# Cross-attention and FP4 FFN on one core: O evicted by VectorE without bias products, eight residual adds and three strips on GpSimd, Sqrt table ahead of Va

## The chip, the cores and the metric

The kernel runs on one core of a Trainium2 chip. The metric is the device time of one execution in microseconds, and the time before is the median of three runs. The engines are named as in the profile: PE (TensorE), DVE (VectorE, `V` in the code), ACT (ScalarE, `A`), POOL (GpSimd, `G`) and SP (SyncE, which here only issues DMAs).

## The reference

The input is 64 sequences of 128 positions with 256 features. With x and the context ctx, both f32, the reference is in short:

```python
# attention over time shifts, weights shared by all sequences
q, k, v = (layernorm(x) @ Wq + bq), (ctx @ Wq + bq), (ctx @ Wq + bq)   # 16 features each
corr = mean(ifft(fft(q) * conj(fft(k))))            # one number per shift
w, shift = softmax(top_k(corr, 12))
R = sum_i w_i * roll(v, -shift_i)                   # along the 128 positions
x = x + repeat(R, 16 heads) @ Wout + bout
# FFN with blockwise FP4 quantisation (blocks of 16 along the last axis)
n = layernorm(x)
h = silu(fp4(n) @ fp4(w_gate).T) * (fp4(n) @ fp4(w_up).T)      # 704 wide
x = x + fp4(h) @ fp4(w_down).T
```

`fp4` divides each block of 16 by its largest magnitude over 6 (but not by less than 1e-12), snaps to the FP4 grid and multiplies back. The top-k takes floor(2 ln 512) = 12 shifts. The attention's result does not depend on all 64 sequences separately: the heads repeat one head, so what is added to x before the FFN is, per group of rows, one 128x256 matrix O.

## The kernel before, in words

**Layout.** The 8192 rows are 64 tiles of 128 rows and 256 features. Four tiles make a quad `X[q]` (128x4x256, f32), loaded by one DMA; quad q has its own `O[q % 4]`, so there are four matrices O, each 128x257 (the last column is a row mean for the layer norm).

**Stages.** Until about 53 us the context, x and the weights are loaded, q, k and v are projected and correlated, and the weights are quantised. Then comes the transition that the change is about, and from 72 us the FFN of tile after tile.

**The transition.** Top-k and softmax run on DVE. ACT fetches the exponentials `E`. The shift weights are turned into a matrix `Wp` (two halves, 128x257): half 0 is started by DVE, half 1 by ACT (L1552, `t1_op`), and both are finished by DVE (L1559). The projected values are transformed by PE into the PSUM tile `pa` and copied by ACT to `Va`, one copy of 128x256 for each of the four groups (L1504). Before the change the planner lets ACT load the Sqrt table (L1553) behind the first of these copies. Then O[g] = Va[g] times Wp over the sum of the exponentials (`inv`), plus the output bias `Bo`:

- O[0] is two matmuls into `pdc` (L1581) and an eviction on DVE that multiplies by `inv` and adds `Bo` (L1594).
- O[1] to O[3] begin with a product of `es` with `Bo` (L1572), a matmul with one row that puts the bias times the sum of exponentials into PSUM, and go on with the two matmuls (L1581). ACT evicts them with the scale `inv` (L1588). All three use the tile `pa`, at other offsets.

**From O to the FFN's input (`x_parts`, L426).** For quad q: `neg` is the negative row mean (L461); the residual X += O is added (L447 on DVE, two tiles at a time; for quads from 3 on, L483, a DMA from the GpSimd queue that accumulates in memory, one for each tile); `cc` = X + neg (L499 on ACT). The first two tiles (`fast`) take cc = X + neg + O in one DVE instruction (L472) and have the add behind it. Then the squares are summed (L509 on ACT), block maxima `am` taken (L519 on DVE), the roots computed (two Sqrt on ACT, L535 and L542, for quads 0 and 1; a polynomial on DVE, L408 to L424, for the others), `am` is floored and scaled (L552, L562), cc multiplied by the reciprocals (L586), snapped to the grid (`k`, L594 or L600 and L607, then L338), and split in two f16 parts `xhl` (L573, L579, L615). `xhl` is transposed to `xT`: for quad 0 by PE with a copy by DVE (tiles 0, 1) or ACT (tiles 2, 3) (L631, L637), for the others by a DMA (L644).

**The FFN of a tile (`group_ops`).** Eighteen matmuls (L1224) make gate and up in one of two PSUM tiles `pg` (called `gu` in the profile), ACT takes silu(gate) (`g`, L1230), DVE multiplies by up (`h`, L1237), reduces block maxima (`hs`, L1247) and their reciprocals (`hr`, L1261), GpSimd multiplies h by hr (`z`, L1276; tiles 0, 62 and 63 on DVE), ACT rounds (L1304, L1320), DVE snaps (L338) and makes the two f16 parts `hl` (L1329), a DMA transposes them, PE multiplies by the down weights (L1373, L1375), DVE adds to X (L1392), and a DMA stores. The reduction for hs also reads two strips beside h in the same tile, 2x88 columns filled once with the least scale (`least`): before the change ACT writes them, once for each of the three buffers of h (L1605).

**What sets the order.** All instructions are first noted by `op(engine, cost, function, reads, writes, dl=...)`, where cost is the author's estimate in ns and `dl` a due time; then a list scheduler (class `Order`) picks, on each engine, among the instructions that are ready the one due first, and writes them out. Each engine executes its list in that order, and waits by semaphores. A due time is handed back to all that an instruction depends on, so a change of one cost or due time shifts the order later on too. `chain` forces an instruction to follow another on the same engine at once: from tile 2 on, hr of tile t-1, h and hs of tile t come one after another on DVE, and the z of tile t-1 on GpSimd, which waits for that hr, runs beside that h and hs. `after` orders without a wait. PSUM waits are per tile: an instruction that writes any part of `pa` waits for earlier readers of `pa`.

On GpSimd the list before is short: after the set-up come the DMAs that accumulate O in quads 3 and 4 (five issues between 73.5 and 78.1 us), then z of tile 1, and from there a z and an accumulating DMA for a later tile (`BEFORE` = 16 tiles ahead) in turn.

Of the kernel before, what the change touches and what calls it, by code (L numbers as in the profile page):

```python
# [18 lines left out]
AF = mybir.ActivationFunctionType  # L19
ALU = mybir.AluOpType  # L20
# [3 lines left out]
P = 128  # L24
D = 256
NF = 704
NB = NF // 16
# [65 lines left out]
class Order:  # L93
# [11 lines left out]
    def op(self, eng, cost, fn, r=(), w=(), dl=1e9, lat=0, after=(), rel=0.0, port=True, late=0.0):  # L105


        o = Op()
        o.port, o.chain, o.late = port, None, late
        o.eng, o.cost, o.fn, o.dl, o.lat, o.n = eng, cost, fn, dl, lat, len(self.ops)  # L110
        o.rel = max(rel, self.rel)
        o.deps, o.succ, o.end, o.bufs, o.after = set(), [], None, set(), set(after)
        for k in r:
            if k in self.last_w:
                o.deps.add(self.last_w[k])
        for k in w:
            if k in self.last_w:
                o.deps.add(self.last_w[k])
            o.deps.update(self.readers.get(k, ()))
        for k in r:  # L120
            self.readers.setdefault(k, set()).add(o)
        for k in w:
            self.last_w[k] = o
            self.readers[k] = set()
        for k in (*r, *w):
            b = k[0] if isinstance(k, tuple) else k
            if isinstance(b, Buf) and b not in o.bufs:
                o.bufs.add(b)
                b.ops.append(o)
        o.deps.discard(o)  # L130
        self.ops.append(o)
        return o
# [128 lines left out]
def xattn_ffn(ctx: ExitStack, tc: tile.TileContext, x, xt, cx, wo, bo, wgu, wd, out):  # L261
    nc = tc.nc
    PE, V, A, G, SP = nc.tensor, nc.vector, nc.scalar, nc.gpsimd, nc.sync
# [4 lines left out]
    op = S.op  # L268
# [5 lines left out]
    O = [res.tile([P, D + 1], F32, name=f"O{g}") for g in range(4)]  # L274
# [59 lines left out]
    def load_x(q, **kw):  # L334
        return op("SP", 1460, lambda: SP.dma_start(X[q].t, x[:, q]), w=[(X[q], i) for i in range(4)] + (["XA"] if q in (6, 7) else []), lat=LL, **kw)
# [4 lines left out]
    SLOT = 5425.0  # L340
# [18 lines left out]
    LL = 1100.0  # L359
    LA = 4000.0  # L360
    BEFORE = 16
    HOT2 = 70000.0
    ZV, CV, EV = (0, *range(62, 64)), range(61, 64), range(64)
    HPE = (63,)
# [35 lines left out]
    def x_stage(*a, **kw):  # L400
        for _ in x_parts(*a, **kw):
            pass
# [23 lines left out]
    def x_parts(R, q, i0, nt, fast, due, alu, pe_x=False, root=False, both=None, off=0):  # L426
# [11 lines left out]
        def cv():  # L438
            return sub("k").bitcast(F16)

        eng = "V"
        pe = fast

        def add(lo, hi):
            def f():
                v = Xq.t[:, i0 + lo : i0 + hi]
                (V if eng == "V" else G).tensor_tensor(v, v, O[g][:, 0:D].unsqueeze(1).broadcast_to([P, hi - lo, D]), ALU.add)  # L447

            n = hi - lo
            op(  # L450
                eng,
                (60 + 270 * n) if eng == "V" else 650 * n if n == 1 else 613 * n,
                f,
                r=[("O", g)],
                w=[(Xq, i0 + i) for i in range(lo, hi)],
            )
# [8 lines left out]
            w=[T["neg"]],  # L465
        )
        for i in tiles:
            if fast:
                op(
                    "V",  # L470
                    336,
                    lambda i=i: V.scalar_tensor_tensor(  # L472
                        T["cc"].t[:, i], Xq.t[:, i0 + i], T["neg"].t[:, i : i + 1], O[g][:, 0:D], ALU.add, ALU.add
                    ),
                    r=[(Xq, i0 + i), T["neg"], ("O", g)],
                    w=[(T["cc"], i)],
                )
        if alu == "D":
            for i in tiles:
                adds[4 * q + i] = op(  # L480
                    "G",
                    900,
                    lambda i=i: G.dma_start(Xq.t[:, i0 + i], O[g][:, 0:D], accum_op=ALU.add),  # L483
                    r=[("O", g)],
                    w=[(Xq, i0 + i)],
                    lat=LA,
                    port=False,
                )
                adds[4 * q + i].rel = 0.0
        else:  # L490
            step = 1 if nt == 1 else 2
            for lo in range(0, nt, step):
                add(lo, lo + step)
        for i in tiles:
            if not fast:
# [702 lines left out]
    def group_ops(tiles):  # L1198
# [16 lines left out]
        for i, t in enumerate(tiles):  # L1215
# [47 lines left out]
                w=[(B["r"], i)],  # L1263
                port=False,
            )
            if t - 1 in recips:
                recips[t - 1].deps.add(g_op)
                recips[t - 1].chain, h_op.chain = h_op, red_op
                h_op.after.add(recips[t - 1])
# [152 lines left out]
    def heat_buf(buf, dl=1e9):  # L1422
        heat(lambda: buf.t[:, 0:P], buf, dl, buf)
# [129 lines left out]
    op("A", 1300, lambda: A.activation(warm, c_half, AF.Sqrt), w=["tbl"], dl=TO, after=[*quick, t1_op])  # L1553
    for e in range(2):
        key, t = spec["B", e]
        w_op = op(
# [5 lines left out]
        )  # L1562
    d_parts(loaded, (w_op,))
    load_x(1, dl=TD + 9000, after=loaded)
    for g in range(4):
        po, pn = ((pdc, "o"), lambda: pdc.t[:, 0 : D + 1]) if g == 0 else ((pa, "o", g), lambda g=g: pa.t[:, 512 * (3 - g) :][:, 0 : D + 1])
        Vg = Va[:, g].rearrange("p (b r e) -> p e (b r)", b=16, e=2)
        if g:
            op(
                "PE",  # L1570
                690,
                lambda pn=pn: PE.matmul(pn(), es[0:1, 0:1].broadcast_to([1, P]), Bo[0:1], start=True, stop=False),  # L1572
                r=["Bo", "es"],
                w=[po],
                after=quick_o,
            )
        first = [
            op(
                "PE",
                560,  # L1580
                lambda e=e, pn=pn, Vg=Vg, g=g: PE.matmul(pn(), Vg[:, e], Wp[:, e], start=(g == e == 0), stop=(e == 1)),  # L1581
                r=[("Va", g), ("Wp", e)],
                w=[po],
            )
            for e in range(2)
        ]
        if g:
            op("A", 450, lambda g=g, pn=pn: A.activation(O[g], pn(), AF.Copy, scale=inv), r=[po, "inv"], w=[("O", g)], dl=TG if g < 2 else TG + SLOT)  # L1588
        else:
            quick_o = first  # L1590
            op(
                "V",
                450,
                lambda pn=pn: V.scalar_tensor_tensor(O[0], pn(), inv, Bo, ALU.mult, ALU.add),  # L1594
                r=[po, "inv", "Bo"],
                w=[("O", 0)],
                dl=TG,
            )

    heat(lambda: hot.t[:, 384:512], (hot, "h"), TG + 7000.0, hot, after=first)  # L1600
    for t in h_tiles:
        op(
            "A",
            350,
            lambda t=t: A.activation(  # L1605
                t[:, :, NF : NF + 2 * NB], ones[:, 0 : 2 * NB].unsqueeze(1).broadcast_to([P, 2, 2 * NB]), AF.Copy, scale=htiny
            ),
            r=[("O", 3)],
            w=["least"],
        )  # L1610
    S.rel = 0.0
    for i, n, e in FIRST:
        x_stage(R4, 0, i, n, True, TG + i * STEP0, e, True, True)
    x_stage(R4, 0, 2, 2, False, TG + 2 * STEP0, "V", True, True)

    X_homes += [xs.tile([P, 4, D], F32, name=f"X{n}") for n in range(2, 6)]
    X_homes += [XA[:, n * 4 * D : (n + 1) * 4 * D].rearrange("p (t d) -> p t d", t=4) for n in range(2)]
# [3 lines left out]
        b.ring = Xr  # L1621
    X += [Xr.new() for _ in range(14)]
    for i, n, d, p in Q1:
        x_stage(R4, 1, i, n, False, TG + DUE1 + d, "V", p, True)
    op("A", 1300, lambda: A.activation(warm, c_half, AF.Silu), w=["tbl"], dl=TG)
# [87 lines left out]
```

## Time and profile before

| what | value |
|---|---|
| median of three runs | 438.35 us |
| the three runs | 436.62, 438.35, 438.74 us |
| the profiled execution: own time | 436.5 us |
| its span, first to last instruction | 434.6 us |
| PE busy | 418.9 us, 96% of the span |
| DVE busy | 392.9 us, 90% |
| ACT busy | 285.6 us, 66% |
| POOL busy | 137.3 us, 32% |
| add X += O, 128x512, on DVE (L447) | 6 times 0.68 us |
| eviction of O, 128x257: DVE (L1594), ACT (L1588) | 0.49 us once, 0.47 us three times |
| strips (L1605), ACT | 3 times 0.44 us |
| table load, ACT | 1.28 us each |
| z on GpSimd, 128x704 (L1276) | 61 times 1.52 us |

Times are in microseconds from the start of the span. A line of the timeline gives start, duration (of the whole group where it ends in x2 or more), engine, line, operation, output <- inputs and shape; brackets hold how long the engine sat idle before and what released it. `PEld` is the weight load of a matmul. The busy shares are means over stages that are limited by different engines, so a stretch has to be read by itself.

### The profile page before, as it was taken

Reading aid. Unit: us, or ns where it says so; the run is one execution under the profiler, and the core shown is the slowest. Engines: PE = TensorE matmul, PEld = TensorE weight load, DVE = VectorE, ACT = ScalarE, POOL = GpSimd, SP = SyncE. Lnnn points to the kernel's source line nnn. Section 1 sums busy time; section 2 is a strip of 40 time slices with the busy share of each in tenths; the row PEclk is TensorE's granted clock in tenths of the full one; section 3 lists DMA queues with packets and bytes.
Section 4 is the critical chain, followed back from the end, with each engine's and each line's share of the span. In section 5 each row is a group of like instructions: output and inputs, shape, how many; then the busy total and the mean of one; then the engine's idle time right before and its main releaser. Section 6 shows DMA issues by size and latency. Waiting matters only on the chain.

```text
span 434.6 us, 7990 instructions
## 1 busy us (share of the span) xinstructions
PE 418.9 (96%) x2946; PEld 268.9 (62%) x2946; DVE 392.9 (90%) x855; ACT 285.6 (66%) x480; POOL 137.3 (32%) x122
## 2 busy tenths in 40 slices
PE   8999989899889999999999999999999999999996
PEld 8557666446555656666566666666665666566685
DVE  7999597999999999899999989999999999978862
ACT  3897557978595787467856794887579576364410
POOL 1000002154344354444444444454444222314100
PEclk9999996999999999999999999999999999999999
DMA  8999999453887688489758987697669716942462
GB/s 309 416 419 419 306 224 321 61 111 79 169 151 147 162 179 190 112 134 241 148 121 165 210 141 172 144 160 157 128 151 173 147 40 133 189 116 66 103 162 74
DMA packets 152247, 76.62 MB, mean 176 GB/s; under 512 B 134160, under 2 KB 141712, under 8 KB 152208
## 3 DMA queue, kind: packets, MB, share of 16 engines
q1 hardware_dynamic: 144720, 69.29, 62.5%
q0 software_dynamic: 7488, 6.82, 11.0%
q8 instruction: 23, 0.38, 0.4%
q14 instruction: 16, 0.13, 0.1%
HBM read 27.76 MB, written 8.39 MB: 83 GB/s over the span
## 4 chain that ended last, share of the span: by engine, by line
PE 66%; DVE 16%; ACT 8%; DMA 6%; issue 2%; SPq 1%; ACTq 0%
PE gu L1224 37%; PE pd L1373 14%; PE pd L1375 8%; DMA xt<-in_xt_dram 4%; DVE hs L1247 3%; DVE h L1237 2%; DMA ct<-in_cx_dram 2%; DVE hl L1329 2%; ACT junk L509 1%; ACT g L1230 1%; ACT cc L499 1%; DVE am L519 1%; DVE cc L586 1%; PE gu L1581 1%; ACT hk L1304 1%
## 5 line engine op out<-in xcount | busy, mean ns | idle before, releaser
L1224 PE MATMUL gu<-WgH,xT 128*128 128x512 f16 (+1 forms) x768 | 191.7, 361 | 5.1 <-ACT g L1230 1.9
L1224 PEld LDWEIGHTS <-xT 128*128 128x128 f16 x1152 | 112.4, 98 | 114.5 <-issue 5.1
L1276 POOL TENSOR_TENSOR h<-h,hr 128x704 f32<-128x704 f32 x61 | 92.6, 1519 | 196.3 <-DVE hr L1261 169.3
L1224 PE MATMUL gu<-WgL,xT 128*128 128x512 f16 (+1 forms) x384 | 107.4, 361 | 0.0
L1230 ACT ACTIVATE g<-gu,ug 128x704 f32<-128x704 f32 x64 | 53.7, 840 | 42.0 <-PE gu L1224 41.9
L1304 ACT ACTIVATE hk<-h,c_half 128x1408 int16<-128x1408 f32 (+1 forms) x34 | 47.4, 1395 | 37.3 <-POOL h L1276 34.4
L1247 DVE TENSOR_REDUCE hs<-h 128x44 f32<-128x792 f32 x64 | 66.6, 1041 | 2.1
L1237 DVE SCALAR_TENSOR_TENSOR h<-gu,uh,g 128x704 f32<-128x704 f32 x64 | 55.9, 874 | 5.1 <-ACT g L1230 3.2
L483 POOL DMA_DIRECT2D X<-O x36 | 31.7, 970 | 71.7 <-ACT junk L509 71.7
L1320 ACT ACTIVATE hc<-hk,c_sub 128x1408 f16<-128x1408 int16 (+1 forms) x32 | 45.6, 1426 | 0.5
L1373 PE MATMUL pd<-WdH,hT 128*128 128x256 f16 x352 | 43.7, 273 | 1.2 <-DMA hT<-hl 1.2
L1373 PEld LDWEIGHTS <-hT 128*128 128x128 f16 x352 | 34.3, 98 | 9.5 <-DMA hT<-hl 1.6
L1329 DVE TENSOR_TENSOR hl<-hc,hsb 128x1408 f16<-128x1408 f16 (+1 forms) x34 | 28.6, 842 | 0.2
L1329 DVE TENSOR_TENSOR hl<-hc,hsl 128x1408 f16<-128x1408 f16 (+1 forms) x34 | 28.6, 841 | 0.0
L1261 DVE RECIPROCAL hr<-hs 128x44 f32<-128x44 f32 x64 | 26.8, 418 | 0.2
L509 ACT ACTIVATE junk<-cc 128x256 bf16<-128x256 f32 x64 | 26.0, 406 | 0.4 <-DVE cc L472 0.2
L1375 PE MATMUL pd<-WdL,hT 128*128 128x256 f16 x192 | 26.2, 273 | 0.0
L1290 ACT ACTIVATE hsb<-hs 128x176 bf16<-128x176 f32 (+1 forms) x34 | 11.4, 334 | 19.8 <-DVE hs L1247 19.8
L499 ACT ACTIVATE cc<-X,neg 128x256 f32<-128x256 f32 x46 | 22.5, 499 | 2.9 <-DVE neg L461 2.9
L932 ACT ACTIVATE xsq<-xt,shift 128x1024 f32<-128x1024 f32 x16 | 17.7, 1142 | 8.9 <-DVE shift L928 6.3
L586 DVE TENSOR_TENSOR cc<-cc,rz 128x256 f32<-128x256 f32 x64 | 23.3, 418 | 0.1
L1373 PE MATMUL pd<-WdH,Wdn 128*128 128x256 f16 x176 | 21.8, 273 | 0.7 <-DMA Wdn<-hl 0.7
(254 smaller groups left out, 569.4 us busy)
## 6 DMA issues: line engine op xcount, KB each, us to landing
xt<-in_xt_dram SPq DMA_DIRECT2D x16, 512.0 KB, 8.2
ct<-in_cx_dram SPq DMA_DIRECT2D x7, 1024.0 KB, 12.8
X<-in_x_dram SPq DMA_DIRECT2D x12, 512.0 KB, 4.4
out_dram<-X SPq DMA_DIRECT2D x23, 256.0 KB, 2.3
X<-O POOLq DMA_DIRECT2D x36, 128.0 KB, 3.4
XA<-in_x_dram SPq DMA_DIRECT2D x4, 512.0 KB, 5.3
XA<-O POOLq DMA_DIRECT2D x16, 128.0 KB, 2.7
out_dram<-XA SPq DMA_DIRECT2D x7, 256.0 KB, 2.0
```

The costliest lines, as they stand in the source:

```text
L483: lambda i=i: G.dma_start(Xq.t[:, i0 + i], O[g][:, 0:D], accum_op=ALU.add),
L509: lambda i=i: A.activation(T["junk"].t, T["cc"].t[:, i], AF.Square, accum_out=T["ssq"].t[:, off + i : off + i + 1]),
L1224: PE.matmul(pg.t[:, c0:c1], src[:, b], w[:, k, c0:c1], start=(m == 0), stop=(m == 5))
L1230: lambda pg=pg, g=g: A.activation(g.t, pg.t[:, 0:NF], AF.Silu, scale=ug),
L1237: lambda pg=pg, g=g, i=i: V.scalar_tensor_tensor(B["h"].t[:, i, 0:NF], pg.t[:, NF:NG], uh, g.t, ALU.mult, ALU.mult),
L1247: lambda i=i: V.tensor_reduce(B["s"].t[:, i], B["h"].t[:, i].rearrange("p (jj b e) -> p b jj e", b=NB, e=2), AX.XY, ALU.max, apply_absolut ...
L1276: lambda i=i, zv=zv: (V if zv else G).tensor_tensor(per_block(B["h"].t[:, i, 0:NF], NB), per_block(B["h"].t[:, i, 0:NF], NB), spread(B["r" ...
L1304: lambda: A.activation(sub("k"), sub("h")[:, :, 0:NF], AF.Identity, bias=c_half, scale=24.0),
L1320: lambda: A.activation(flat("c"), flat("k"), AF.Identity, bias=c_sub, scale=SUB),
L1329: lambda e=e, part=part: V.tensor_tensor(B["hl"].t[:, 0:nt, e].rearrange("p t (jj n) -> p t jj n", jj=JJ), sub("c").rearrange("p t (jj n) ...
L1373: PE.matmul(pd, hT.t[:, b], WdH[:, :, b], start=(b == 0), stop=False)
L1375: PE.matmul(pd, hT.t[:, b], WdL[:, :, b], start=False, stop=(b == 5))
```

## The change

- The products with `Bo` (L1572) are gone. All four O are evicted by DVE with `O = PSUM * inv + Bo` (`scalar_tensor_tensor`), due at TG, TG + 3000 and twice TG + 12000 ns; the matmuls of group g are ordered behind those of group g - 1.
- `x_parts` knows a new kind `alu="P"`: the add X += O is done by GpSimd, one tile of 128x256 at a time. It is used for tiles 0 to 3 (`A0`, `A2`) and, by `Q2A`, for tiles 8 to 11 (quad 2). Quad 1 keeps its two adds on DVE; quads from 3 on keep the accumulating DMAs.
- The three strips are written by GpSimd (`tensor_scalar`, ones times `htiny`). A row of `after` edges fixes GpSimd's order: adds of tiles 2, 3, 0, 1, 8, 9, the three strips, adds of 10, 11, then the DMAs of X3 and X4.
- The Sqrt table is due 12 us sooner and no longer ordered behind the first Va copy; it comes out ahead of all four copies. The Silu table is due 4 us later.
- The forced sequence hr, h, hs on DVE holds from tile 6 on (`CHAIN`) rather than from tile 2.
- Options that stay unused here (`cce`, `C1`, `C2E`, `F2`) come along. The planner's order differs at many places from the transition to the end; nine heater matmuls stand behind the O products where three stood before, and on SP five neighbouring issues change places.

```diff
+    OD = 3000.0
+    DQ = 2
+    GORD = (4, 5, 6, 7, 2, 3, 0, 1, 8, 9, 10, 11)
+    LEAST = 5
+    CHAIN = 6
+    Q2A = "P"
+    A0 = "P"
+    A1 = "V"
+    A2 = "P"
+    DUE2 = 7200.0
+    SILU = 4000.0
+    GA = 800.0
...
-        eng = "V"
+        eng = "G" if alu == "P" else "V"
...
-            op(
+            adds[4 * q + i0 + lo] = op(
                 eng,
-                (60 + 270 * n) if eng == "V" else 650 * n if n == 1 else 613 * n,
+                (60 + 270 * n) if eng == "V" else GA * n,
...
-            step = 1 if nt == 1 else 2
+            step = 1 if nt == 1 or eng == "G" else 2
...
-            if t - 1 in recips:
+            if t - 1 in recips and t >= CHAIN:
...
-    op("A", 1300, lambda: A.activation(warm, c_half, AF.Sqrt), w=["tbl"], dl=TO, after=[*quick, t1_op])
+    op("A", 1300, lambda: A.activation(warm, c_half, AF.Sqrt), w=["tbl"], dl=TO - 12000.0, after=[t1_op])
...
-        if g:
-            op(
-                "PE",
-                690,
-                lambda pn=pn: PE.matmul(pn(), es[0:1, 0:1].broadcast_to([1, P]), Bo[0:1], start=True, stop=False),
-                r=["Bo", "es"],
-                w=[po],
-                after=quick_o,
-            )
...
+                after=quick_o,
             )
             for e in range(2)
         ]
-        if g:
-            op("A", 450, lambda g=g, pn=pn: A.activation(O[g], pn(), AF.Copy, scale=inv), r=[po, "inv"], w=[("O", g)], dl=TG if g < 2 else TG + SLOT)
-        else:
...
+        quick_o = first
+        op(
+            "V",
+            450,
+            lambda g=g, pn=pn: V.scalar_tensor_tensor(O[g], pn(), inv, Bo, ALU.mult, ALU.add),
+            r=[po, "inv", "Bo"],
+            w=[("O", g)],
+            dl=(TG, TG + OD, TG + 12000.0, TG + 12000.0)[g],
+        )
...
-    for t in h_tiles:
-        op(
-            "A",
-            350,
...
+    least = [
+        op(
+            "G",
+            500,
+            lambda t=t: G.tensor_scalar(
+                t[:, :, NF : NF + 2 * NB], ones[:, 0 : 2 * NB].unsqueeze(1).broadcast_to([P, 2, 2 * NB]), htiny, None, ALU.mult
             ),
             w=["least"],
+            after=first,
+            dl=TG + 12000.0,
+        )
+        for t in h_tiles
+    ]
...
-        x_stage(R4, 0, i, n, True, TG + i * STEP0, e, True, True)
-    x_stage(R4, 0, 2, 2, False, TG + 2 * STEP0, "V", True, True)
+        x_stage(R4, 0, i, n, True, TG + i * STEP0, A0, True, True)
+    x_stage(R4, 0, 2, 2, F2, TG + DUE2, A2, P2, True, cce=C2E)
...
-    op("A", 1300, lambda: A.activation(warm, c_half, AF.Silu), w=["tbl"], dl=TG)
+    op("A", 1300, lambda: A.activation(warm, c_half, AF.Silu), w=["tbl"], dl=TG + SILU)
...
-            parts.append((due, x_parts(R4, q, 0, 4, False, due, "D" if q > 2 else "V", both=both, off=4 * n)))
+            parts.append((due, x_parts(R4, q, 0, 4, False, due, "D" if q > DQ else Q2A, both=both, off=4 * n)))
...
+    row = [adds[t] for t in (*GORD, *range(12, 17)) if t in adds and adds[t].eng == "G"]
+    for o, u in zip(row, row[1:]):
+        u.after.add(o)
+    for o in least if len(row) > 5 else ():
+        o.after.add(row[LEAST])
+        row[LEAST + 1].after.add(o)
```

More of the change, by code (lines that the diff above doesn't have):

```diff
@@ L361, in xattn_ffn @@
     BEFORE = 16
+    OD = 3000.0
[7 more added lines that the diff above has]
+    A2 = "P"
+    C1 = None
+    C2E = None
+    F2 = False
+    P2 = True
+    DUE2 = 7200.0
+    SILU = 4000.0
+    GC = 1060.0
+    GA = 800.0
     HOT2 = 70000.0
@@ L424, in roots, with x_parts @@
         op("V", 75, lambda: V.scalar_tensor_tensor(t, v, TINY / 4.0 / -3.2, y, ALU.mult, ALU.mult), r=[bv, by], w=[bt])
-    def x_parts(R, q, i0, nt, fast, due, alu, pe_x=False, root=False, both=None, off=0):
+    def x_parts(R, q, i0, nt, fast, due, alu, pe_x=False, root=False, both=None, off=0, cce=None):
         g, hq = q % 4, q // 4
@@ L467, in x_parts @@
         for i in tiles:
-            if fast:
+            if fast or cce == "V":
                 op(
@@ L479, in x_parts @@
             for i in tiles:
-                adds[4 * q + i] = op(
+                adds[4 * q + i0 + i] = op(
                     "G",
@@ L488, in x_parts @@
                 )
-                adds[4 * q + i].rel = 0.0
+                adds[4 * q + i0 + i].rel = 0.0
         else:
-            step = 1 if nt == 1 else 2
+            step = 1 if nt == 1 or eng == "G" else 2
             for lo in range(0, nt, step):
@@ L494, in x_parts @@
         for i in tiles:
-            if not fast:
+            if cce == "G":
+                op(
+                    "G",
+                    GC,
+                    lambda i=i: G.tensor_scalar(
+                        T["cc"].t[:, i], Xq.t[:, i0 + i], T["neg"].t[:, i : i + 1], None, ALU.add
+                    ),
+                    r=[(Xq, i0 + i), T["neg"]],
+                    w=[(T["cc"], i)],
+                )
+            elif not fast and cce != "V":
                 op(
@@ L1564, in xattn_ffn @@
     load_x(1, dl=TD + 9000, after=loaded)
+    quick_o = ()
     for g in range(4):
@@ L1580, in xattn_ffn @@
                 560,
-                lambda e=e, pn=pn, Vg=Vg, g=g: PE.matmul(pn(), Vg[:, e], Wp[:, e], start=(g == e == 0), stop=(e == 1)),
+                lambda e=e, pn=pn, Vg=Vg, g=g: PE.matmul(pn(), Vg[:, e], Wp[:, e], start=(e == 0), stop=(e == 1)),
                 r=[("Va", g), ("Wp", e)],
                 w=[po],
+                after=quick_o,
             )
@@ L1586, in xattn_ffn @@
         ]
-        if g:
-            op("A", 450, lambda g=g, pn=pn: A.activation(O[g], pn(), AF.Copy, scale=inv), r=[po, "inv"], w=[("O", g)], dl=TG if g < 2 else TG + SLOT)
-        else:
-            quick_o = first
-            op(
[L1592 to L1598, printed above, removed]
+        quick_o = first
[7 more added lines that the diff above has]
+        )
     heat(lambda: hot.t[:, 384:512], (hot, "h"), TG + 7000.0, hot, after=first)
-    for t in h_tiles:
+    least = [
         op(
-            "A",
-            350,
-            lambda t=t: A.activation(
-                t[:, :, NF : NF + 2 * NB], ones[:, 0 : 2 * NB].unsqueeze(1).broadcast_to([P, 2, 2 * NB]), AF.Copy, scale=htiny
+            "G",
+            500,
+            lambda t=t: G.tensor_scalar(
+                t[:, :, NF : NF + 2 * NB], ones[:, 0 : 2 * NB].unsqueeze(1).broadcast_to([P, 2, 2 * NB]), htiny, None, ALU.mult
             ),
-            r=[("O", 3)],
             w=["least"],
-        )
+            after=first,
+            dl=TG + 12000.0,
+        )
+        for t in h_tiles
+    ]
     S.rel = 0.0
     for i, n, e in FIRST:
-        x_stage(R4, 0, i, n, True, TG + i * STEP0, e, True, True)
-    x_stage(R4, 0, 2, 2, False, TG + 2 * STEP0, "V", True, True)
+        x_stage(R4, 0, i, n, True, TG + i * STEP0, A0, True, True)
+    x_stage(R4, 0, 2, 2, F2, TG + DUE2, A2, P2, True, cce=C2E)
     X_homes += [xs.tile([P, 4, D], F32, name=f"X{n}") for n in range(2, 6)]
@@ L1623, in xattn_ffn @@
     for i, n, d, p in Q1:
-        x_stage(R4, 1, i, n, False, TG + DUE1 + d, "V", p, True)
-    op("A", 1300, lambda: A.activation(warm, c_half, AF.Silu), w=["tbl"], dl=TG)
+        x_stage(R4, 1, i, n, False, TG + DUE1 + d, A1, p, True, cce=C1)
+    op("A", 1300, lambda: A.activation(warm, c_half, AF.Silu), w=["tbl"], dl=TG + SILU)
     for qs in QS:
```

## The prediction

> **What bounds the kernel now.** I read the busy shares first, then a table of busy time by stretch, then the timeline of the stretch that the change touches. The table's columns are span, busy time (and instructions) of PE, PEld, DVE, ACT, POOL, then the granted clock, the DMA share and GB/s.
>
> ```profile
> 69.00:72.00 3.00, 2.93 (x15) 2.32 (x14) 0.46 (x2) 1.92 (x6) 0.00 (x0) 0.50 0.97 355
> 72.00:80.00 8.00, 7.90 (x42) 3.79 (x43) 7.86 (x24) 7.88 (x21) 4.54 (x5) 0.98 1.05 280
> 80.00:90.00 10.00, 7.95 (x48) 4.46 (x46) 9.93 (x19) 9.28 (x22) 0.03 (x1) 1.00 0.24 54
> 100.00:120.00 20.00, 18.07 (x113) 10.74 (x112) 19.62 (x51) 14.32 (x30) 7.04 (x6) 1.00 0.59 122
> 120.00:140.00 20.00, 18.24 (x114) 10.91 (x113) 19.53 (x40) 16.27 (x31) 9.35 (x8) 1.00 0.82 158
> 200.00:420.00 220.00, 219.74 (x1420) 138.83 (x1419) 204.48 (x393) 144.91 (x229) 83.00 (x67) 1.00 0.71 146
> ```
>
> Three regimes are to be seen. From 200 us TensorE never rests (219.74 of 220), so whatever puts it ahead by then is kept to the end. Between 72 and 140 VectorE is the one without a gap (7.86 of 8, 9.93 of 10, 19.62 and 19.53 of 20), ScalarE is full too up to 90, and TensorE waits: 2.05 us in 80 to 90, 1.93 and 1.76 in the next two. From 69 to 72 the reverse: VectorE is busy 0.46 of 3 us, at half the granted clock on TensorE. The timeline tells why (start, busy, engine, line, operation; in brackets idle time and what ended it):
>
> ```profile
> 59.78 0.37 ACT L1504 COPY Va<-gu 128x256 f32<-128x256 f32 x1 [1.23 <-PE gu L1495]
> 60.17 1.28 ACT L1553 ACT_TABLE_LOAD   x1
> 61.39 0.49 DVE L1594 SCALAR_TENSOR_TENSOR O<-pd,inv,Bo 128x257 f32<-128x257 f32 x1
> 62.53 0.69 PE L1572 MATMUL gu<-Bo,es 1*128 1x257 f32 x2 [1.18 <-ACT Va L1504]
> ...
> 66.46 0.48 ACT L1588 ACTIVATE O<-gu,inv 128x257 f32<-128x257 f32 x1 [2.19 <-PE gu L1581]
> 66.99 1.22 PE L1572 MATMUL gu<-Bo,es 1*128 1x257 f32 x2
> 68.00 0.69 DVE L447 TENSOR_TENSOR X<-X,O 128x512 f32<-128x512 f32 x1
> 68.14 2.08 PE L1581 MATMUL gu<-Wp,Va 128*128 128x257 f32 x4
> 70.26 0.84 ACT L1588 ACTIVATE O<-gu,inv 128x257 f32<-128x257 f32 x2 [1.08 <-PE gu L1581]
> 71.54 0.42 DVE L637 COPY xT<-pd 128x512 f16<-128x512 f16 x1 [2.86 <-PE pd L631]
> 72.02 0.70 PE L1224 MATMUL gu<-WgH,xT 128*128 128x512 f16 x2
> 75.38 1.28 ACT L1625 ACT_TABLE_LOAD   x1
> 80.50 1.89 DVE L447 TENSOR_TENSOR X<-X,O 128x512 f32<-128x512 f32 x3
> ```
>
> VectorE had the first two tiles ready to transpose at 67.95 (xhl). TensorE was still in the products for O2 and O3, which stood behind ScalarE's eviction of O1, and got to the transposes at 70.87. VectorE lost 2.86 us and the first FFN product began at 72.02.
>
> **The change, part by part.** The sum is made against the profiled execution: 436.5 us of its own, span 434.6. The runs shown have a median of 438.35, 1.85 above it.
>
> *Sqrt table ahead of the Va copies.* ScalarE is free after Wp (58.56), so load and warm-up (1.28 + 0.20) run in the 1.23 us in which it waited, and end near 60.1; the first copy ends near 60.6 instead of 60.15, the other three follow at once instead of at 61.58. O0's matmul and eviction, and VectorE's queue behind them, are late by 0.5 us. **+0.5.**
>
> *Bias products out, O1 to O3 on VectorE.* Six matmul rows of L1572 go (0.69 + 0.70 + 1.22 = 2.6 us of TensorE, the last pair at half clock), and the two stops for ScalarE's eviction with them. A new wait stands there: O3's last matmul waits for VectorE's eviction of O1. Queued behind it are the transposes, and VectorE itself waits for those; but that eviction is early in VectorE's order. Six products at about 0.43 each plus the heater matmuls let TensorE go at 65.5 to 67, so VectorE is late next, not TensorE: its xhl. VectorE's wait goes, **-2.86**; three evictions arrive at 0.46 (the row of L1594 has 0.49, and the next operation starts somewhat before such an end), **+1.4**.
>
> *Adds to GpSimd.* VectorE loses four of its six adds of 128x512 (those at 63.83 and 68.00 and two of the three from 80.50), at a pitch of 0.60 to 0.63: **-2.5**. GpSimd gets eight of 128x256. No such add is in the trace; its 128x704 product takes 1.52 us, so in proportion 0.55, and 0.87 at the top, which is the dispatch of its DMAs: 4.4 to 7 us between 62 and 76, where POOL did 4.54 us of DMA issues. On its queue the add of tile 8 waits for X2's load and O2, and behind it stand the strips, tiles 10 and 11, the four X3 and four X4 accumulating DMAs and all later products z. The load was issued at 62.91, and such loads landed 4 to 8 us later, so by 71: not late. hs of tile 0 needs the strips; they are done by 76, and hs began at 82.31. X3's DMAs move from 73.5 to about 76 and are wanted after 100; that costs nothing. On SyncE's queue five neighbouring issues change places; no wait that the timeline shows between 59 and 84 ended with a DMA, so these cost nothing either.
>
> *ScalarE.* It loses three evictions (0.47) and three strips (0.44), 2.7 us out of 66 to 82, where it has no gap. That brings Silu's table (75.38) and g of tile 0 (78.29) forward, and shortens the 2.05 us TensorE waited in 80 to 90. VectorE's own gain is counted already; beyond it I take **-0.5**, between 0 and -1.0.
>
> *Collisions.* Now GpSimd's adds run beside VectorE operations with two inputs in SBUF (cc, am times t, cc*rz, slo), and with the chain from tile 6 only, the products z of tiles 1 to 4 are no longer placed beside h and hs. Only one pair in the trace shows such a meeting:
>
> ```profile
> 365.87 1.52 POOL L1276 TENSOR_TENSOR h<-h,hr 128x704 f32<-128x704 f32 x1 [4.12 <-DVE hr L1261]
> 367.18 0.36 DVE L579 TENSOR_TENSOR slo<-am,shb 128x128 f16<-128x128 f32 x1
> ```
>
> The small subtraction, 0.29 in the mean, took 0.36, with 0.21 of it beside the product: 0.07 lost, a third of the overlap, or none, since these spread. If each excluded the other wholly, I count, going through both queues in order, 1.0 to 1.9 us at the adds of tiles 0 to 3 (at 0.6 and 0.8 an add), 1.2 to 1.5 at tiles 8 to 11, and 1.2 to 2.3 at the four z. So the price lies between 0 and 5.7. The one row that shows the case is nearest: a third. **+1.1** for the adds (of 3.4), **+0.5** for the z (of a middle of 1.7).
>
> The Trainium skill ("SBUF — State Buffer", Who interferes with whom) speaks against this change: VectorE and GpSimd share a port pair, a VectorE instruction with two SBUF inputs contends with a GpSimd one that reads SBUF, and the lock holds for the whole instruction. The row above agrees that there is a loss and is too small to show whether it is whole. By that rule the 5.7 is paid in place of 1.6, and the sum would be +1.7 us, slower than before.
>
> Sum: 0.5 - 2.86 + 1.4 - 2.5 - 0.5 + 1.1 + 0.5 = **-2.4 us**, own time 434.1. It is earned before 90 us and kept where TensorE is the bound. Everything later is ordered anew by the planner; TensorE waits only 1.2 us from 140 to 420, so a better order wins no more than that, and a worse one may lose as much. The runs shown and the profiled one have a mean 1.5 above 436.5, the median 1.85; with 1.6 the time is **435.7**.
>
> **The rivals.**
> *Collisions take it all (slower).* One mechanism: GpSimd holds VectorE's two-input operations for its whole instruction, at the places counted above. With the adds at 0.87 the price is 6.3 (2.2 + 1.8 + 2.3), and ScalarE's half microsecond is worth nothing while VectorE is the bound: 0.5 - 2.86 + 1.4 - 2.5 + 6.3 = +2.8, 439.3 of its own, 441 as a median. It decides from 3.5 us lost on. For it: VectorE has no gap in 72 to 140 to lose time in, and since z stands beside h and hs nearly everywhere, the trace shows almost nothing of its price. Against it: the one meeting seen; and between 74 and 79 VectorE works ahead of a g of tile 0 that ScalarE holds, which covers part.
>
> *The start is not the limit (same).* The first FFN product comes 2 us sooner, but g of tile 0 waits for ScalarE's queue and the Silu load, now due later, or the half clock (0.50 from 66 to 72) falls on the first FFN products instead of on the O products. Then the 2.86 is not won: 0.5 + 1.4 - 2.5 - 0.5 + 1.6 = +0.5, and as some of the collisions then fall into the wait, 436.5 to 437.0 of its own, a median of 438.3. For it: ScalarE busy 7.88 of 8. Against: it loses 2.7 us there.
>
> *No collision at all (faster).* The 1.6 is not paid and the second 0.5 of ScalarE is: 434.1 - 2.1 = 432.0, median 433.6. For it: cc and the evictions are spread over few microseconds; against: the row above.
>
> *The adds come late on GpSimd.* At 0.87 each and in series, tiles 2 and 3 would hold ScalarE's cc by 1 us; ScalarE has other work then. Inside the range.
>
> **How the numbers follow.** Half a per cent, 2.2 us, is about what a measurement of this kernel can tell from no change (its runs span 2.1). Chances: the sum as told 0.46 (434 to 437), collisions take it all 0.28 (439 to 442), the start is not the limit 0.16 (437 to 439.5), no collision 0.10. Faster (below 436.2): most of the first, all of the last, a little of the third: 0.53. Slower (above 440.5): three quarters of the second: 0.22. Same: the rest of these, 0.25. The range, 432.5 to 441, leaves out the upper half of the second case and little below.
>
> **What would show it.** Right: first L1224 matmul at 69.5 to 70.5; no wait of 2 us on VectorE before L637; ScalarE with gaps before 80; h of tile 0 near 77.5 and h of tile 4 two to three us before 96.65; TensorE's idle time in 72 to 140 under 5.8. Wrong: cc, am*t or cc*rz on VectorE at two or three times their 0.48, 0.18 and 0.42 while GpSimd adds; L1276 above 1.6; hs of tile 0 waiting for the strips; a TensorE gap before h's products of tiles 3 to 6; or VectorE's evictions of O2 and O3 waiting for products held by ScalarE's late Va copies.

## The result and the profile after

The changed kernel is slower: a median of 439.58 us (438.78 to 440.06, 11 runs) against 437.40 us (434.88 to 438.74, 11 runs) for the kernel before in the same comparison, a ratio of 1.0051 with a 95% interval of 1.0035 to 1.0068. The profiled execution took 439.76 us of its own, span 437.8. The time of the kernel before depends more on the clock granted to TensorE: in the three comparisons made later, its executions with a mean clock of 1.00 took 434.3 to 434.9 us in the mean (four in each) and those at 0.988 took 437.7 to 438.1, while the changed kernel's took 438.9 at 1.00 (four) and 439.9 at 0.992 (four). At a full clock the loss is thus about 4 us, more than the 2.2 between the medians.

The table of busy time by stretch of the changed kernel, with the columns as before (span; busy time and instructions of PE, PEld, DVE, ACT, POOL; granted clock, DMA share, GB/s):

```profile
69.00:72.00 3.00, 2.70 (x19) 1.94 (x19) 2.50 (x8) 1.81 (x6) 0.14 (x1) 0.81 1.01 371
72.00:80.00 8.00, 7.25 (x42) 3.57 (x40) 7.90 (x22) 6.62 (x16) 8.00 (x11) 1.00 0.51 171
80.00:90.00 10.00, 8.47 (x45) 4.45 (x46) 9.90 (x19) 8.52 (x19) 3.39 (x4) 1.00 0.77 143
100.00:120.00 20.00, 17.50 (x104) 10.33 (x103) 19.71 (x42) 14.97 (x31) 7.16 (x6) 0.91 0.49 105
120.00:140.00 20.00, 18.05 (x115) 10.97 (x114) 19.73 (x47) 15.67 (x30) 9.28 (x8) 1.00 0.80 172
200.00:420.00 220.00, 217.96 (x1400) 136.69 (x1398) 204.14 (x390) 145.20 (x228) 84.54 (x68) 1.00 0.70 141
```

VectorE's pause between 69 and 72 is gone (2.50 busy where it was 0.46), and ScalarE has air before 80 (6.62 of 8 where it was 7.88). But VectorE is still full from 72 to 140, GpSimd is now busy all of 72 to 80, TensorE waits longer than before in 100 to 140, its clock drops there (0.91), and 2.0 us are lost between 200 and 420 where 0.26 was.

What VectorE did with the time is in its timeline. Its rows, and below them GpSimd's, of the changed kernel in the transition:

```profile
62.44 1.70 DVE L489 SCALAR_TENSOR_TENSOR cc<-X,neg,O 128x256 f32<-128x256 f32 x2
...
64.78 0.65 DVE L478 TENSOR_SCALAR neg<-MT,O 128x2 f32<-128x2 f32 x1
...
71.94 1.19 DVE L464 TENSOR_TENSOR X<-X,O 128x512 f32<-128x512 f32 x1
```
```profile
62.23 3.18 POOL L464 TENSOR_TENSOR X<-X,O 128x256 f32<-128x256 f32 x4 [60.42 <-DVE O L1611]
71.86 1.86 POOL L464 TENSOR_TENSOR X<-X,O 128x256 f32<-128x256 f32 x2 [6.45 <-ACT junk L536]
73.70 2.64 POOL L1622 TENSOR_SCALAR h<-ones,htiny 128x176 f32<-128x176 f32 x3
76.31 1.46 POOL L464 TENSOR_TENSOR X<-X,O 128x256 f32<-128x256 f32 x2
```

The two cc take 1.70 us where they took 0.88 before, and neg of two columns 0.65 where it took 0.22; the add of 128x512, 0.68 alone, takes 1.19. The row of cc in the kernel before:

```profile
62.18 0.88 DVE L472 SCALAR_TENSOR_TENSOR cc<-X,neg,O 128x256 f32<-128x256 f32 x2
```

Each ends at, or some tenths of a microsecond after, the end of the GpSimd add that it met: the adds started at 62.23 with a pitch of 0.80, so they ended near 63.0, 63.8, 64.6 and 65.4, and neg ended at 65.43. GpSimd is held in its turn: the second of the adds at 71.86 began at 72.54, beside VectorE's add of 128x512, and took 1.18 us where the first took 0.73. VectorE is held in the same way later, at the products z of tiles 1 to 4, which no longer stand beside h and hs:

```profile
89.55 1.03 DVE L1324 SCALAR_TENSOR_TENSOR hsl<-hs,hsb 128x88 f16<-128x88 f32 x1
...
93.68 0.93 DVE L338 TENSOR_SCALAR hc<-hc 128x704 int16<-128x704 int16 x1
...
95.32 1.85 DVE L1356 TENSOR_TENSOR hl<-hc,hsl 128x704 f16<-128x704 f16 x1
...
102.51 1.27 DVE L338 TENSOR_SCALAR hc<-hc 128x1408 int16<-128x1408 int16 x1
```

```profile
88.95 1.52 POOL L1303 TENSOR_TENSOR h<-h,hr 128x704 f32<-128x704 f32 x1 [6.61 <-DVE hr L1288]
92.89 1.52 POOL L1303 TENSOR_TENSOR h<-h,hr 128x704 f32<-128x704 f32 x1 [1.60 <-DVE y L429]
95.11 1.67 POOL L1303 TENSOR_TENSOR h<-h,hr 128x704 f32<-128x704 f32 x1
101.88 1.51 POOL L1303 TENSOR_TENSOR h<-h,hr 128x704 f32<-128x704 f32 x1 [4.27 <-DVE t L441]
```

Alone these four take 0.24, 0.33, 0.52 and 0.52 us; in the kernel before, the row of hl is:

```profile
95.81 0.52 DVE L1329 TENSOR_TENSOR hl<-hc,hsl 128x704 f16<-128x704 f16 x1
```

hl at 95.32 ended at 97.17, 0.39 us after the product beside it. Worked out as a loss: 0.8 + 0.6 + 1.3 + 0.75 = 3.5 us at the z, and 0.8 (cc) + 0.4 + 0.4 (neg, at 64.78 and 76.42) + 0.5 (add) + 0.1 (am times y, beside a strip) = 2.3 us at the adds; 5.8 us of VectorE in all.

TensorE's waits show what it came to. The row of its first FFN product, and those that ended its longest waits from there on:

```profile
70.97 0.61 PE L1251 MATMUL gu<-WgH,xT 128*128 128x512 f16 x2 [0.30 <-DVE xT L664]
107.78 1.01 PE L1251 MATMUL gu<-WgH,xT 128*128 128x512 f16 x2 [2.50 <-DVE h L1264]
136.75 0.60 PE L1251 MATMUL gu<-WgH,xT 128*128 128x512 f16 x2 [1.95 <-DMA xT<-xhl]
291.55 0.48 PE L1251 MATMUL gu<-WgH,xT 128*128 128x384 f16 x2 [1.13 <-ACT g L1257]
361.18 0.48 PE L1251 MATMUL gu<-WgH,xT 128*128 128x384 f16 x2 [0.85 <-ACT g L1257]
```

The first product started 1.05 us sooner than before. h of tile 1 was 0.98 us ahead of before (85.22 against 86.20), h of tile 3 only 0.64, h of tile 4 2.04 behind (98.69 against 96.65): the z stand between. The wait of 2.50 us at 107.78 is one for VectorE, and two products behind it take 1.01 us instead of 0.59: the clock was at half for some 3 us.

### The profile page after: what moved, and what is told of

Same layout as the page of the kernel before. It is cut to its first block, busy times and chain, and to the rows that moved or that the text cites. A ratio compares the mean times of both kernels' runs of the same rounds, so it can differ in the third digit from the quotient of the medians.

```text
span 437.8 us, 8002 instructions
## 1 busy us (share of the span) xinstructions
PE 417.9 (95%) x2950; PEld 268.0 (61%) x2950; DVE 397.2 (91%) x854; ACT 284.3 (65%) x474; POOL 147.3 (34%) x133
## 4 chain that ended last, share of the span: by engine, by line
PE 64%; DVE 18%; DMA 9%; ACT 5%; issue 2%; SPq 1%; POOL 0%; ACTq 0%
PE gu L1251 38%; PE pd L1400 14%; PE pd L1402 7%; DMA xt<-in_xt_dram 6%; DVE hs L1274 2%; DVE hl L1356 2%; DVE h L1264 2%; DMA ct<-in_cx_dram 2%; DVE cc L613 2%; DMA xT<-xhl 1%; ACT hk L1331 1%; ACT g L1257 1%; DVE am L546 1%; PE gu L753 1%; ACT hc L1347 1%
## 5 line engine op out<-in xcount | busy, mean ns | idle before, releaser
L1251 PE MATMUL gu<-WgH,xT 128*128 128x512 f16 (+1 forms) x768 | 193.7, 363 | 9.6 <-DVE h L1264 4.8
L1264 DVE SCALAR_TENSOR_TENSOR h<-gu,uh,g 128x704 f32<-128x704 f32 x64 | 56.8, 887 | 6.8 <-ACT g L1257 4.7
L1356 DVE TENSOR_TENSOR hl<-hc,hsl 128x1408 f16<-128x1408 f16 (+1 forms) x34 | 29.8, 877 | 0.0
L464 POOL TENSOR_TENSOR X<-X,O 128x256 f32<-128x256 f32 x8 | 6.5, 838 | 66.9 <-DVE O L1611 60.4
L627 ACT ACTIVATE k<-cc,c_half 128x1024 int16<-128x1024 f32 (+1 forms) x16 | 17.9, 1118 | 13.0 <-DVE cc L613 13.0
L338 DVE TENSOR_SCALAR hc<-hc 128x1408 int16<-128x1408 int16 (+1 forms) x34 | 18.3, 539 | 6.3 <-ACT hc L1347 6.0
```

Of the source, the lines that this page charges most:

```text
L1251: PE.matmul(pg.t[:, c0:c1], src[:, b], w[:, k, c0:c1], start=(m == 0), stop=(m == 5))
L1264: lambda pg=pg, g=g, i=i: V.scalar_tensor_tensor(B["h"].t[:, i, 0:NF], pg.t[:, NF:NG], uh, g.t, ALU.mult, ALU.mult),
L1356: lambda e=e, part=part: V.tensor_tensor(B["hl"].t[:, 0:nt, e].rearrange("p t (jj n) -> p t jj n", jj=JJ), sub("c").rearrange("p t (jj n) ...
```

## The experiments

All medians below stand beside the kernel before on the same chip (437.1 to 437.4 in the three sets). "In the same order" means that the planner saw the changed kernel's costs, and only what is issued in one place differs; what waited for the part left out can then come sooner.

**The forced sequence from tile 2, in the changed kernel (`e1_chain2`).**

```diff
-    CHAIN = 6
+    CHAIN = 2
```

> The changed kernel, with hr, h and hs forced together from tile 2 on again instead of from tile 6, and planned anew. Theory C (collisions at the products z of tiles 1 to 4): in the changed kernel hsl, hc and hl beside these products took 1.03, 0.93 and 1.85 us where they took 0.24, 0.33 and 0.52 alone, 2.7 us lost; with z beside h and hs again these go, and the time falls by 1.5 to 2.7 us, to 437 to 438. Rival O (the later order alone makes the difference, through gaps at 291 and 361 us): these long forms vanish too, but the time stays within 1 us of 439.6 or moves without relation to them.

438.98 us, ratio 1.0050 (1.0029 to 1.0071). The long forms at z are gone, but the time is only 0.6 below the changed kernel: by its number this run falls to rival O. Its gaps at 291 and 361 us are not the reason, though, since they are absent here too (from 200 to 420 us this kernel loses 0.25 us). The trace shows another one: h of tile 6 came 2.8 us sooner than before (104.32 against 107.12), and then TensorE waited for tile 8's input:

```profile
114.84 1.03 PE L1251 MATMUL gu<-WgH,xT 128*128 128x512 f16 x2 [7.96 <-DMA xT<-xhl]
```

Quad 2's xhl ended at 109.6, one microsecond sooner than before, and its transposing DMA was issued behind one for hl; what was gained up to there was lost in one wait. TensorE also had nothing else to do meanwhile: in this order the down products of tiles 2 and 3 come behind tile 8 (117.38), and their hl was made only from 106.36 to 108.38.

**The forced sequence from tile 6, in the kernel before (`e2_before_chain6`).**

```diff
-            if t - 1 in recips:
+            if t - 1 in recips and t >= 6:
```

> The kernel before, with one part of the change alone: the forced sequence from tile 6 on. Theory C: operations with two inputs in SBUF come to stand beside z of tiles 1 to 4 and are held; 1 to 2.7 us slower than before, 438.4 to 440. Rival O: within 1 us of before, on either side.

441.91 us, ratio 1.0105 (1.0071 to 1.0140): 4.8 us slower from this part alone, more than expected. Even operations of four columns are held in this run:

```profile
98.84 1.48 DVE L418 SCALAR_TENSOR_TENSOR p<-t 128x4 f32<-128x4 f32 x1
103.40 1.16 DVE L424 SCALAR_TENSOR_TENSOR t<-ssq,y 128x4 f32<-128x4 f32 x1
```

Each takes 0.16 in the kernel before, and z stood beside them (98.75 to 100.30, 103.02 to 104.53). Two more were held, a tensor_scalar (ssq, L408, 0.81 instead of 0.16) and an hl (0.93 instead of 0.52), so 3.4 us of VectorE in all. The rest of the 4.8 is not accounted for operation by operation; TensorE's longest wait in it is 3.60 us, before 113.97.

**GpSimd's adds left out, same order (`e4_no_g_adds`).**

```diff
-                (V if eng == "V" else G).tensor_tensor(v, v, O[g]..., ALU.add)
+                if eng == "V":
+                    V.tensor_tensor(v, v, O[g]..., ALU.add)
```

> The changed kernel in the same order on every engine, with GpSimd's eight adds left out, so tiles 0 to 3 and 8 to 11 miss their residual O in X (the output is wrong there). Theory C, at the adds: cc of tiles 0 and 1, two neg, am*y and the add of quad 1 fall back to their lone durations, 2.3 us less on VectorE between 62 and 77; the first FFN product at 69.5 to 70 instead of 70.97, the whole 1 to 2 us faster than the changed kernel. Rival S (the start is covered by ScalarE and the Silu load): first FFN product sooner, but g of tile 0 as before near 78.4 and the end within 0.7 us.

436.22 us, 3.4 below the changed kernel (ratio to before 0.9990, 0.9970 to 1.0010). cc takes 0.88 for two again, neg 0.22, the add 0.68; the first FFN product starts at 69.16 and h of tile 0 at 77.25, 2.8 us sooner than in the changed kernel, and the profiled span is 3.2 shorter. Some of that is the clock: in the profiled execution of the changed kernel it was at half from 66.7 to 70.1 us and in this one it was not. Two other runs with the same work up to there but without that clock (e1 and e5) have h of tile 0 at 79.03, but they were ahead already at the first O product (60.03; the changed kernel 60.47, this run 60.52). Counted from there, h of tile 0 comes after 19.6 us in the changed kernel, 19.0 in e1 and e5, and 16.7 here: 0.6 us is the clock and 2.3 the adds, as much as the durations say. Without the adds GpSimd's later work comes sooner too (the strips at 58.29 instead of 73.70, X3's DMAs at 72.92 instead of 77.72); none of the waits in the changed kernel from 70 to 140 us ended with these. Rival S, a start that ScalarE covers, is out.

**z of tiles 1 to 4 left out, same order (`e5_no_z`).**

```diff
-                lambda i=i, zv=zv: (V if zv else G).tensor_tensor(
+                lambda i=i, zv=zv, t=t: None if 1 <= t <= 4 else (V if zv else G).tensor_tensor(
```

> The changed kernel in the same order on every engine, with the products z of tiles 1 to 4 on GpSimd left out (the output of these tiles is wrong). Theory C: hsl, hc and hl at 88 to 97 us take 0.24, 0.33 and 0.52; h of tile 4 comes 2.5 us sooner, TensorE's wait of 2.5 us before 107.78 shrinks and so does the half clock behind it; 2 to 4 us faster than the changed kernel. Rival O: h of tile 4 comes sooner, but the end moves by less than 1 us, since the gaps at 291 and 361 remain.

436.75 us, 2.8 below the changed kernel (ratio to before 0.9999, 0.9977 to 1.0021). hsl takes 0.24, hc 0.34 and 0.46, hl 0.51, h of tile 4 comes at 95.53 (98.69 in the changed kernel), and the half clock at 108 us is absent (one of the same length, 3.4 us, stands at 133.4). The row of hl:

```profile
93.51 0.51 DVE L1356 TENSOR_TENSOR hl<-hc,hsl 128x704 f16<-128x704 f16 x1
```

Of the 3.2 us at tile 4, 1.0 stood there already at tile 0 (79.03 against 80.06: the clock and an earlier start), so 2.1 are due to z up to there and 2.9 by tile 5 (102.81 against 106.78). Leaving z out also takes a step of 1.52 us out of the way from h to ScalarE's rounding. That isn't what helped: VectorE has no gap in the changed kernel from 80 to 107 us (29.82 busy of 30 in 80 to 110), so only time of VectorE itself could bring h forward there. Theory C holds. The gaps of rival O are there too, unchanged (1.14 us at 288, 0.86 at 358): they belong to the changed kernel's order and are 1.7 us of its time, but they are not what sets this run apart.

**Both left out (`e6_neither`).**

> The changed kernel in the same order, with both left out: GpSimd's eight adds and the products z of tiles 1 to 4 (those tiles' output is wrong). Theory C (the collisions are the whole difference): the two savings add up, 439.6 - 3.4 - 2.8 = 433.4, some 3.5 us faster than before. Rival W (another wall stands behind them, such as the transposed inputs of tiles 8 on): less than one of the two is added to 436.2, so 435 to 436.5.

433.53 us, ratio 0.9916 (0.9886 to 0.9946). By the medians the two savings add up to within 0.2 us; by the ratios to before they are 2.7 and 2.3 us and together 5.9, so within 1 us. In the medians this is 4 us faster than before. The run leaves out the work itself and not only the collisions, so it is a bound for the changed kernel without them and no version.

**The eight adds on VectorE in the same places (`e7_adds_on_v`).**

```diff
-                (V if eng == "V" else G).tensor_tensor(v, v, O[g]..., ALU.add)
+                V.tensor_tensor(v, v, O[g]..., ALU.add)
```

> The changed kernel in the same order, GpSimd's eight adds of 128x256 given to VectorE at the same places. By theory C the adds on GpSimd cost VectorE 2.3 us (measured at cc, neg, am*y and the add of quad 1), and on VectorE they cost eight times about 0.37, 2.9 us: within 1 us of the changed kernel, 439.5 to 440.5. Rival L (collisions are cheap against the adds, the loss lies in the order and in z): 2 us or more slower than the changed kernel.

438.98 us, ratio 1.0044 (1.0026 to 1.0061), which overlaps the changed kernel's. Handing eight adds to GpSimd bought nothing measurable: VectorE stood still for them about as long as it would have added.

**The sequence from tile 2 and quad 2 sooner (`f1_q2_early`).**

```diff
-    CHAIN = 6
+    CHAIN = 2
...
-            due = T0 + SLOT * (4 * q - min(MARGIN, LEAD[0] + LEAD[1] * q))
+            due = T0 + SLOT * (4 * q - min(MARGIN, LEAD[0] + LEAD[1] * q)) - (9000.0 if q == 2 else 0.0)
```

> The changed kernel with the forced sequence from tile 2 again and the input of quad 2 (tiles 8 to 11) due 9 us sooner, planned anew. In the run with the sequence alone, TensorE ran 2.8 us ahead at tile 6 and then waited 7.96 us for the transposed input of tile 8, at half clock for 3 us behind it. Theory Q (the order of quad 2 is what ate the gain there): that wait shrinks below 4 us and the time falls to 433 to 436, below both kernels. Rival V (VectorE's sum of work sets it, wherever it is put): the wait moves elsewhere and the time stays at 438 to 439.5.

435.30 us, ratio 0.9958 (0.9937 to 0.9978): faster than both kernels. Between executions of like mean clock (0.991 to 0.996) the lead on the kernel before is 1.5 us (435.3 in the mean of 12, 436.9 of 14). The wait for tile 8's input is 2.93 us instead of 7.96:

```profile
112.06 0.60 PE L1251 MATMUL gu<-WgH,xT 128*128 128x512 f16 x2 [2.93 <-DMA xT<-xhl]
```

**The part around O alone (`e8_o_part`).**

```diff
-    CHAIN = 6
-    Q2A = "P"
-    A0 = "P"
-    A2 = "P"
+    CHAIN = 2
+    Q2A = "V"
+    A0 = "V"
+    A2 = "V"
```

> The changed kernel with all adds on VectorE and the forced sequence from tile 2 on, planned anew: of the change there remain O's evictions on VectorE without bias products, the Sqrt table ahead of Va, the strips on GpSimd. By the terms of the sum: +0.5 - 2.9 + 1.4 - 0.5 = -1.5 against before, so about 435.5, with the order's own spread of 1 to 2 us. Rival (the start is not the limit): 437 to 438.

438.76 us, ratio 1.0039 (1.0015 to 1.0063). The expectation missed, and the trace says how: h of tile 7 came at 108.51, 5.0 us ahead of before (113.52), and h of tile 8 at 126.62, 3.7 behind it (122.88). Between them lies one stop:

```profile
117.82 2.53 PE L1400 MATMUL pd<-WdH,Wdn 128*128 128x256 f16 x11 [7.24 <-DVE am L579]
```

It stands ahead of tile 4's down product, which reads the transposed hl of tiles 4 and 5 (kept in the tile called Wdn) and not the am that the row names. VectorE made that hl from 112.59 to 114.62, behind quad 2's cc times rz (110.35), though ScalarE had finished hc at 108.96; the transposing DMA was issued at 114.65. Quad 2 itself was late as well: its xhl ended at 116.89, 6.1 us later than before (110.78).

**Two controls for the due time:** quad 2 due 9 us sooner in the kernel before (`c1_before_q2`) and in the changed kernel (`c2_after_q2`), nothing else. Both have the line with `due` of the run f1 and not its `CHAIN`.

> The kernel before, with quad 2's input due 9 us sooner and nothing else: the control for the run with the forced sequence and the earlier quad 2, which took 435.3 against 437.4 before. Theory Q2 (the earlier start is worth 2 to 3 us once quad 2 no longer stops it): the kernel before gains nothing from an earlier quad 2, as its TensorE waits only 0.69 us for that input, 437 to 438. Rival D (the due time alone is what helped): 435 to 436.

437.57 us, ratio 1.0005 (0.9974 to 1.0035): nothing, though the wait for that input did not stay at 0.69 us but grew to 2.74 (113.13), about as long as in f1. The due time alone is not what made f1 fast. With quad 2 sooner in both, f1 differs from this control by the change without its loose z: 435.30 against 437.57, 2.3 us faster.

> The changed kernel with quad 2's input due 9 us sooner, the forced sequence still from tile 6 only. Theory C: collisions of the products z of tiles 1 to 4 stay, some 2 to 3 us slower than the same with the sequence from tile 2 (435.3), so 437.5 to 438.5. Rival D (the due time alone): 435 to 436.

441.69 us, ratio 1.0102 (1.0065 to 1.0140): 6.4 above f1, from which it differs only by the forced sequence. The direction is theory C's, the size was expected at 2 to 3. This order puts costlier pairs beside the four z; the rows:

```profile
88.45 1.46 DVE L425 TENSOR_SCALAR ssq<-ssq 128x4 f32<-128x4 f32 x1
...
95.62 1.48 DVE L441 SCALAR_TENSOR_TENSOR t<-ssq,y 128x4 f32<-128x4 f32 x1
...
99.30 2.68 DVE L613 TENSOR_TENSOR cc<-cc,rz 128x256 f32<-128x256 f32 x4
...
109.80 2.20 DVE L1356 TENSOR_TENSOR hl<-hc,hsl 128x1408 f16<-128x1408 f16 x1
```

Alone they take 0.15, 0.15, 1.42 and 0.88, so 5.2 us are lost here.

**Without GpSimd's adds, quad 2 sooner (`f2_adds_v_q2`), and with quad 2's adds as accumulating DMAs (`f3_dma_q2`).** f2 is e8 with the line with `due` of f1; f3 has in addition:

```diff
-    DQ = 2
-    LEAST = 5
+    DQ = 1
+    LEAST = 0
```

> All adds on VectorE, forced sequence from tile 2, quad 2's input due 9 us sooner. The same without the earlier quad 2 ran 5.0 us ahead of before at tile 7 and lost it in one wait of 7.24 us before 117.82. If GpSimd's adds are worth nothing net, 434.5 to 436, the same as with GpSimd's adds (435.3) within 1 us; if they do relieve VectorE by 2 us, 437 or more.

435.83 us, ratio 0.9976 (0.9953 to 0.9999). Within 0.6 us of the kernel with GpSimd's adds (f1): the second witness that they are worth next to nothing.

> As the run before it, with the adds of tiles 8 to 11 as accumulating DMAs, as quads 3 on have them: VectorE is rid of two adds of 128x512 (1.2 us) and no GpSimd add meets it. 433.5 to 435 if VectorE's work to 140 us sets the time; the same as the run with the adds on VectorE if the DMA's landing (2.7 to 5.5 us) holds quad 2.

434.01 us, ratio 0.9933 (0.9911 to 0.9955): 1.8 us below f2 and the fastest version here that computes the whole result, 3.4 us below the kernel before and 5.6 below the changed kernel. Much of the lead on the kernel before goes with the clock: this version's executions had a mean clock of 0.995 to 1.00, most of the kernel before 0.987 to 0.992. At 1.00 the two took 433.9 (three) and 434.3 us (four), at 0.995 to 0.996 435.2 (four) and 435.8 (five). What keeps its clock up was not tried. Its longest wait of TensorE after 72 us is for tile 8's input, as in f1:

```profile
111.15 0.60 PE L1251 MATMUL gu<-WgH,xT 128*128 128x512 f16 x2 [2.73 <-DMA xT<-xhl]
```

## Why the prediction was wrong

The forecast was 2.4 us faster; it came out 2.2 slower in the medians. Point by point:

- *What bounds the kernel* held: VectorE up to 140 us, TensorE behind. Shifts of VectorE in the frozen order (e4) came through to the end nearly one to one: 2.8 us at tile 0, 3.2 in the span.
- *Sqrt table, +0.5*: the first Va copy ended near 60.4 instead of 60.15 and O[0]'s eviction began at 61.66 instead of 61.39, so +0.3, of which 0.1 stood there already when ScalarE's half of Wp was done (58.65 instead of 58.56).
- *The wait of 2.86 us* went: VectorE waited 0.50 before the xT copy. The new wait on O[1]'s eviction was said to be early in VectorE's order; it was not, and TensorE stood 2.09 us for it (65.88). In e5, which had no half clock there, it was hidden, as the step had it, by VectorE's own late xhl: the transposes waited 0.38 us for it. In the changed kernel's profile the heater products behind the wait ran at half clock, and the transposes began at 69.99, 0.7 us behind xhl's end (69.25). The three evictions took 1.34 us, as forecast (1.4).
- *Adds of 0.55 to 0.87 on GpSimd*: 0.80 in pitch. The strips and the add of tile 8 held nobody, as said.
- *ScalarE* got its air (6.62 of 8 us), and g of tile 0 came at 78.44, no sooner than 78.29: what it gained before 80 VectorE had lost. That ScalarE "has no gap" in 66 to 82 was misread: the row at 70.26 has one of 1.08 us before it.
- ***Collisions: "The one row that shows the case is nearest: a third."*** This is the step that failed. The price was bounded by 0 and 5.7 and taken at 1.6. The durations give 5.8, of which 2.3 at the adds (bound 3.4) and 3.5 at the z (upper bound 2.3); leaving them out gives 3.4 and 2.8 us of time between the medians (2.7 and 2.3 by the ratios). So nearly the whole upper bound was due. The rival "collisions take it all" is what happened, at 5.8 instead of 6.3.
- *The row itself* was misread. In it the subtraction (367.18, 0.36 us) ended 0.15 us after the product (365.87 + 1.52 = 367.39). The loss of 0.07 looked small because the reduction before it filled VectorE until 367.26: the subtraction could lose 0.13 at the most, not 0.21. Judged by its end, it behaved like hl in the changed kernel, which began 1.46 us before the product's end and ended 0.39 after it. One row with 0.13 us at stake couldn't carry a fraction; its end against the product's end could have told whole from partial.
- The Trainium skill ("SBUF — State Buffer", Who interferes with whom) says that the pair is held for the whole instruction. For the adds and the products z the runs agree; for the strips they do not, and the measurement decides (last section). It would have made the sum +1.7 us, and +2.2 was measured in the medians. The page also lists `tensor_scalar` among what can take the pair, and here neg, the int16 snap and ssq (0.15 to 1.46 us) were held; the count of places in the prediction had left these out.
- *The later order*: the bound was about 1.2 us; the gaps at 291 and 361 cost 1.7 more than before. That is a second, smaller miss, and it is in e4 to e6 as well.
- Left out of the sum: with the sequence from tile 2 and a faster start, the planned order around quad 2 becomes the next wall. e1, ahead by 2.8 us, waits 7.96 us for its input, and e8, ahead by 5.0, 7.24 us for an hl made behind its preparation. Being early is not enough for it: e6, in the changed kernel's order, has h of tile 6 at 104.26, as soon as e1 (104.32), and waits only 1.14 us for tile 8's input, with the down products of tiles 2 and 3 (106.14 to 110.02) ahead of tile 8 on TensorE, which in e1 come behind it.

Put together: with 5.8 in place of 1.6 the sum is +1.8 us, and with the 1.7 of the later order +3.5. The two profiled executions, both at a mean clock of 0.992, differ by 3.3 (439.76 against 436.5). The no-collision rival stood at 433.6 and the run without collisions (e6) gave 433.53; that is partly luck, for e6 has the 1.7 us of the later order in it, which the rival did not count, and no run shows what made up for it. (The runs shown lay 1.4 us above 436.5 in the mean, not 1.5 as the forecast has it; that changes nothing.)

## What to carry to other kernels

In these runs a GpSimd operation with two SBUF inputs held VectorE until its end where VectorE had an operation with two SBUF inputs, or a `tensor_scalar` from SBUF to SBUF, that began after it. One that was already under way was not held; then GpSimd's operation took longer (z 1.67, 1.74 and 1.96 us instead of 1.52, beside an hl). So place it beside operations that read PSUM, reductions and reciprocals, or let a DMA add. Where the trace of a tuned kernel shows no collisions, ask what keeps them away, and price the removal of that keeper by the longest pair that can arise, not by the one that happened to. When a gain vanishes between two tiles, look for the input that TensorE waits for there and for what stands ahead of it on the engine that prepares it: its due time may have to move with the gain (f1 against e1: 7.96 us of waiting became 2.93).

## What the runs showed of the hardware beyond this

- A held operation's own size did not matter: four columns waited 1.46 us (0.15 alone) beside a product of 1.53.
- The strips on GpSimd (a `tensor_scalar` of 128x176, 0.71 to 0.77 us alone) held VectorE hardly at all: the two cc*rz beside them took 0.76, as alone, and am times y 0.32 instead of 0.18. Here GpSimd was the one to lose: the second strip, beside these, took 1.18, and in e4 one took 1.41 beside VectorE's products with two SBUF inputs (L798). The GpSimd operations that held VectorE had two SBUF inputs. Whether this or something else makes the difference wasn't tried.
- A short stop can cost TensorE more than itself. After the waits of 2.50 us (changed kernel) and 7.96 us (e1) the granted clock was 0.50 for about 3 us and pairs of products took 1.01 to 1.06 us instead of 0.59; after the waits of 2.93 and 2.73 us in f1 and f3 the first pair took 0.60. The length of the wait alone does not decide it: the wait of 2.50 us stands at the same place in e4 (104.95) and e7 (107.44) with no half clock behind it, and in e5 one of 1.97 us (132.82) has 3.4 us of half clock behind it. At 108 us the half clock cost the changed kernel little: from h of tile 5 to h of tile 8 it took 15.35 us, and e7 15.09, where TensorE, at full clock, waited 1.09 us for tile 8's input instead.
